# Six softmax stages of a two-layer graph network taken in pairs, by Strassen's scheme

## The chip, the cores and the metric

The kernel runs on one core of a Trainium2 chip. The metric is device time in microseconds (us), as the median of some runs. PE is TensorE, DVE VectorE, ACT ScalarE, POOL GpSimd, and SP the engine that only issues DMAs; POOL and ACT issue DMAs too. PEld is the load of a matmul's stationary operand, which PE does beside its matmuls.

## The reference, cut to what matters

There are N = 2048 nodes, a batch of B = 8 and C = 64 features. A layer multiplies the features with N x N matrices ("supports"), mixes the results with weights that differ from node to node, adds the input and normalises. The change is in the last support of layer 1:

```
apt = jax.nn.softmax(jax.nn.relu(node_embeddings @ node_embeddings.T), axis=1)
x_g = jnp.einsum('knm,bmc->bknc', supports, x)     # supports = [I, lap, 2 lap lap - I, apt]
out = jnp.einsum('bnki,nkio->bno', x_g, weights) + bias
```

So apt is a 2048 x 2048 matrix that is made on the chip, and it is multiplied with x of layer 1, which is 2048 x 512 (B times C columns). Everything is in 32-bit floats.

## The kernel before

**Stages.** The work is 5 phases (A0, B0, A1, Z1, V1) of 8 stages each, one stage for NB = 256 nodes, numbered 0 to 39 (line 680). A0 and B0 make layer 0; A1 multiplies adj with x; **Z1, stages 24 to 31, multiplies apt with x**; V1 multiplies adj with A1's result u. In most stages of the other phases the product is made by Strassen's scheme in Winograd's form (`strassen`, line 457): the 256 nodes are two halves of 128, the 2048 inner indices are two interleaved halves, the 512 columns two halves, and seven products of half size stand in place of eight, with sums T1 to T4 of x's quarters (made once, `Sums`, line 645) and sums of the matrix's quarters. A Z1 stage, and the first stages of some phases, are made plainly.

**A Z1 stage.** `scores` (line 601) makes two of the 16 blocks of 128 x 256 entries at a time: two small matmuls (tile ps) of the embeddings s1 with the stage's own embeddings e2; a DVE instruction that takes the greater of 0 and the score and subtracts a node's constant c (128x512); and ACT's exponential. The result p is a numerator of the softmax. `turned` (line 554) then runs 16 x 2 x 2 = 64 matmuls, in the profile pz<-p,x, with x's 128 columns as the stationary operand and p (128x256) as the moving one. Each stage's last step, `turned_half` (line 575), takes the two accumulators out of PSUM into the tile t with four DVE instructions (64x512) that also multiply by the reciprocal of the softmax's sum, the second row of c. Then POOL stores t's upper half (zd). V1's stages read it back later.

**The order of the work.** PE runs its instructions as the program writes them, and so does every other engine. `put(n, place, f)` (line 694) hangs a function on stage n at a place between 0 and 64 of its product; a place is scaled by the stage's length (64 for a Z1 stage; 56 for a Strassen stage, whose `yield`s sum to that). The loop at line 791 draws matmuls from the stage's generator and runs each function when its place is reached. In the Z1 stages the functions are few: scores (line 782), `load_e` of the next stage (line 772; POOL loads e2 in two DMAs and then c), the splitting of weights for V1 (lines 712 to 715, stages 25 to 28: ACT loads, DVE splits, POOL stores to wd), and `load_u` of one block of A1's result into the room u (line 728, place 12, on SP's queue).

**Rooms.** x and u are 16 slabs of 512 floats per partition each. During A1 the room u holds the sums T1 to T4 of x; in Z1 the result u is loaded over them. w_room has 16384 floats per partition for the weights of one stage; from the last use in stage 24 (place 43) to the first weights of stage 32 (place 4) it is empty. e2 and t have two buffers each, c has two, the tile group f2k four. PSUM has two accumulators of one bank (ps_acc) and three two-bank tiles (big) for everything else.

**Queues.** SP's queue holds, in program order, the loads of adj (a), of u, and of the split weights (wst, three buffers, `Ahead` at line 221). A DMA that must wait holds those behind it. In stage 32 the first weights' matmuls (pw<-e,wst) come at place 4.

Of the kernel before, what the change touches and what calls it, by code (L numbers as in the profile page):

```python
# [1 line left out]

# [12 lines left out]
P = 128  # L15
# [32 lines left out]
def two_graph_layers(ctx: ExitStack, tc: tile.TileContext, x, x_t, adj_b, adj_q, layers, out):  # L48
# [40 lines left out]
    def big(name):  # L89
        return ps_big.tile([P, 2, 512], F32, tag="big", name=name)  # L90
# [170 lines left out]
    class Stage:  # L261
        def __init__(self, n, phase, j):
            self.n, self.phase, self.j = n, phase, j
            self.li, self.kk = int(phase[1]), int(phase[0] != "A")
            self.half = phase == "B0"
            self.plain = (phase, j) in plain
            self.length = 64 if self.plain or phase == "Z1" else 56
            self.units = C // 2 if self.half else C
            self.e2 = e2[n % 2]
            self.t = self.sq = None  # L270
            self.dev = {}


        def load_e(self):
            cols = slice(self.j * NB, (self.j + 1) * NB)
            for h in range(2):
                pool.dma_start(out=self.e2[64 * h:64 * h + 64, :].bitcast(F32), in_=estk[self.li][:, cols])
            if self.phase == "Z1":
                self.c = two.tile([P, 2, NB], F32, tag="c", name="c")
                pool.dma_start(out=self.c, in_=cd[self.j].rearrange("k s p -> k (s p)").partition_broadcast(P))  # L280

        def load_acc(self):
# [127 lines left out]


        def product(self):
            if self.phase == "Z1":
                return self.turned(X, self.softmax())
            if self.kk:
                return self.turned(U, self.loaded()) if self.plain else self.strassen(U)
            if self.n == 0:
                self.slabs = U[0:SB]
            else:
                made = one.tile([P, SB, BC], F32, tag="wraw", name="u")  # L420
                self.slabs = [made[:, s, :] for s in range(SB)]
            return self.straight(X) if self.plain else self.strassen(X)
# [34 lines left out]
        def strassen(self, right):  # L457
            half = BC // 2
            k_slab = NJ // 2
            sums = self.sums  # L460
            rights = {"B11": lambda k: right[2 * k][:, 0:half], "B21": lambda k: right[2 * k + 1][:, 0:half],
                      "B22": lambda k: right[2 * k + 1][:, half:BC]}
            for i in range(4):
                rights[f"T{i + 1}"] = lambda k, i=i: sums[i](k)
            temps = one.tile([P, 4, half], F32, tag="wsplit", name="temps")
            p1, p4, v = (temps[:, i, :] for i in range(3))
            made, mine = {}, {}
            inside = self.phase == "A0"

            def quarter(name):  # L470
                mine[name] = adj.next()
                adj.held += 1

            def sum_of_a(i, name, a, b, op):
                dve.tensor_tensor(mine[name], mine[a], mine[b], op=op)
                pool.dma_start(out=sd[self.j][i].rearrange("p k n -> p (k n)"), in_=mine[name])

            def times(name, what, left):
                made[name] = acc = self.accumulator(name)[:, 0:half]
                a = (mine[left] if inside else adj.next()).rearrange("p (k n) -> p k n", n=P)  # L480
                for k in range(k_slab):
                    if self.kk:
                        for q in range(2):
                            pe.matmul(acc[:, q * P:(q + 1) * P], rights[what](k)[:, q * P:(q + 1) * P], a[:, k, :],
                                      start=(k == 0 and q == 0), stop=(k == k_slab - 1 and q == 1))
                            yield 0.5
                    else:
                        pe.matmul(acc, a[:, k, :], rights[what](k), start=(k == 0), stop=(k == k_slab - 1))
                        yield 1
                if inside and name in ("p7", "p6", "p5", "p3"):  # L490
                    adj.held -= 1
                    adj.fill()
                    self.used(what)

            def add(dst, a, b, op=ALU.add):

                if not isinstance(dst, tuple):
                    dve.tensor_tensor(dst, a, b, op=op)
                elif self.kk == 0:
                    dve.tensor_tensor(self.slabs[dst[0]][:, dst[1] * half:(dst[1] + 1) * half], a, b, op=op)  # L500
                else:
                    to = self.features()[0:64, dst[0] * P:(dst[0] + 1) * P, :]
                    for par in range(2):
                        of = lambda x: x[64 * par:64 * par + 64, :].rearrange("p (q n) -> p n q", n=P)
                        dve.tensor_tensor(to[:, :, 4 * dst[1] + par:4 * dst[1] + par + 3:2], of(a), of(b), op=op)

            if inside:
                quarter("A11")
                quarter("A22")
            yield from times("p1", "B11", "A11")  # L510
            act.copy(p1, made["p1"])
            if inside:
                quarter("A21")
                sum_of_a(2, "A11", "A11", "A21", ALU.subtract)
                sum_of_a(0, "A21", "A21", "A22", ALU.add)
            yield from times("p4", "T4", "A22")
            self.used("T4")
            act.copy(p4, made["p4"])
            if inside:
                quarter("A12")  # L520
                sum_of_a(1, "A22", "A22", "A11", ALU.subtract)
            yield from times("p7", "T3", "A11")
            add(v, made["p7"], p1)
            add(p4, v, p4, ALU.subtract)
            yield from times("p2", "B21", "A12")
            add((0, 0), made["p2"], p1)
            if inside:
                sum_of_a(3, "A12", "A12", "A22", ALU.subtract)
            yield from times("p6", "T2", "A22")
            add(v, made["p6"], v)  # L530
            add(p1, made["p6"], p1)
            add((1, 0), made["p6"], p4)
            yield from times("p5", "T1", "A21")
            add(p1, made["p5"], p1)
            add((1, 1), made["p5"], v)
            self.repeat(1)
            yield from times("p3", "B22", "A12")
            add((0, 1), made["p3"], p1)
            self.repeat(0)
            self.store_u()  # L540

        def used(self, what):

            first = {"T4": 0, "T1": 4, "T2": 8, "T3": 12}.get(what)
            if (self.phase, self.j) == ("A0", NBLK - 1) and first is not None:
                load_u(range(first // 2, min(first // 2 + 2, NBLK - 1)))

        def repeat(self, s):

            if self.half:  # L550
                t = self.t[:, s * P:(s + 1) * P, :]
                pool.dma_start(out=t[64:128, :, :], in_=t[0:64, :, :])

        def turned(self, stationary, moving):
# [13 lines left out]
                        self.turned_half(i, accs[i])  # L568
                m0 += len(group)
            if self.phase == "Z1":  # L570
                pool.dma_start(out=zd[self.j], in_=self.t[64:128, :, :])
            for s in range(SB):
                self.repeat(s)

        def turned_half(self, i, acc):
            t = self.features()
            for par in range(2):
# [5 lines left out]
                                      op=ALU.mult)  # L583
                else:
                    copy(par, t[0:64, :, at], src)

        def load_z(self):
            pool.dma_start(out=self.features()[64:128, :, :], in_=zd[self.j])
# [12 lines left out]
        def scores(self, c):  # L601
# [8 lines left out]
                                     op0=ALU.max, op1=ALU.subtract)  # L610
            act.activation(p.rearrange("p m n -> p (m n)"), p.rearrange("p m n -> p (m n)"), AF.Exp)
            self.p[c] = p


        def scores_of_rows(self, s, h):
# [56 lines left out]
    for phase, slabs, room, n in (("B0", u_all, w_room[:, 10240:16384], 3), ("A1", x_all, flat_u, 4),  # L672
                                  ("V1", u_all, flat_x, 3)):
        r = thirds(room, n)
        sums[phase] = Sums(slabs, [r[1], r[2], r[3], r[0]] if n == 4 else [r[0], None, r[1], r[2]])
    sums["A0"] = sums["A1"]

# [1 line left out]
              for j in range(NBLK)]  # L681
    for st in stages:
        st.sums = sums.get(st.phase)
    stages[0].load_e()

    split_rooms = [lambda: one.tile([P, 8, P], F32R, tag="wsplit", name="wsplit"),
# [23 lines left out]
        for part in range(3):  # L710
            put(2 + n, 24 + 5 * part, split_weights, part, *key)
    for c in range(V0 // 8):
        put(25 + c, 10, load_weights, 1, 1, c)
        for part in range(3):
            put(25 + c, 40 + part, split_weights, part, 1, 1, c)
    for i, place in ((0, 51), (3, 54), (2, 60)):
        put(8, place, sums["B0"].make, i)
    put(9, 0, sums["B0"].make, 1)
# [6 lines left out]
    for i, place in ((0, 10), (2, 20), (3, 30)):  # L725
        put(32, place, sums["V1"].make, i)
    put(33, 0, sums["V1"].make, 1)
    for j in range(NBLK):
        put(24 + j, 12, load_u, (j,))

    for n, st in enumerate(stages):
        phase = st.phase
        cuts = (0, 3, 6, 9, 12, 14, 16) if st.units == C else (0, 3, 6, 8)
# [35 lines left out]
            for k, place in enumerate(posts):  # L769
                put(n + 1, place, st.post, k)  # L770
        if n + 1 < len(stages):
            put(n, 44 if n < 23 else 37 if n < 25 else 4, stages[n + 1].load_e)
        if phase[0] == "A":
            put(*((1, 12) if n == 0 else (n, 28) if st.li == 0 else (n, 37)), st.bias)
            if st.li == 0:
# [2 lines left out]
                put(n, 47 if st.j else 57, st.turn, 0, "x")  # L778
        if phase != "Z1":
            put(*((1, 26) if n == 0 else (n, 48 + 6 * st.li) if st.kk == 0 else (n, 30)), st.load_acc)  # L780
        else:
            st.p = [None] * 8
            for c in range(8):
# [75 lines left out]
```

## Time and profile before

| | |
|---|---|
| median of 3 runs | 1505.93 us (1505.57 to 1506.24) |
| the profiled execution's own time | 1506.8 us |
| its span in the profile | 1505.0 us |
| mean granted clock of PE | 0.994 |
| PE busy from 931 to 1181 us (stages 24 to 31) | 249.98 of 250 us |
| DVE busy in the same stretch | 93.25 us |
| PE busy from 1181 us to the end | 310.15 of 324 us |
| matmuls pz<-p,x (the Z1 product) | 1024 records, 232.7 us |

A matmul on 32-bit floats shows as two records: 8 stages of 64 matmuls make the 1024. A row of the groups has the shapes, the count, then the group's busy time and the mean duration of one in ns, and then the idle time of the engine before them with what ended it. Durations of matmuls overlap, so what one costs is read from start to start. The chain of waits walks back from the last instruction to what released each step, and lists the time that each piece adds.

### The profile page before, as it was taken

To read this page: it belongs to the slowest core of one execution; us is meant where nothing else is said; L and a number is where in the kernel's file an instruction comes from. 1 tells how busy PE (TensorE), PEld (TensorE's weight loads), DVE (VectorE), ACT (ScalarE), POOL (GpSimd) and SP (SyncE) were. 2 spreads that over 40 slices of the span, in tenths; PEclk is the share of its full clock that TensorE was granted. 3 is DMA by queue.
4 is the path that set the end of the run, shared out by engine and by line. 5 is a ranking of instruction groups with operands and counts; after the bars stand their busy time and mean duration, and the time that the engine had idled before them with its cause. 6 is when DMAs were issued, how large, how long until landed. Compare 5 with 4: busy or idle time off the path is not lost.

```text
span 1505.0 us, 31332 instructions
## 1 busy us (share of the span) xinstructions
PE 1472.4 (98%) x13406; PEld 1200.7 (80%) x13406; DVE 895.1 (59%) x1599; ACT 475.6 (32%) x608; POOL 206.6 (14%) x343
## 2 busy tenths in 40 slices
PE   9999999999999999999999999999999999999996
PEld 4477777778998898477777777788888888888885
DVE  3876666628666666866666667533432466666665
ACT  1344444431221122144444444311111233333332
POOL 4222222110111111111110111110010000000100
PEclk9999999999999999999999999999999999999998
DMA  9888898874666566478887788532211346656651
GB/s 360 264 265 269 276 281 273 289 285 145 201 201 200 189 206 219 132 182 191 208 179 197 203 175 185 163 106 67 81 41 27 102 152 195 195 194 189 196 194 56
DMA packets 86732, 283.39 MB, mean 188 GB/s; under 512 B 14017, under 2 KB 18113, under 8 KB 84993
## 3 DMA queue, kind: packets, MB, share of 16 engines
q1 hardware_dynamic: 53600, 171.99, 38.5%
q0 software_dynamic: 27520, 95.76, 21.2%
q10 hardware_dynamic: 5472, 13.63, 2.7%
q8 instruction: 106, 1.74, 0.5%
q14 instruction: 34, 0.27, 0.1%
HBM read 216.28 MB, written 60.83 MB: 184 GB/s over the span
## 4 chain that ended last, share of the span: by engine, by line
PE 75%; issue 17%; DVE 3%; POOL 2%; DMA 2%; ACT 1%; POOLq 0%; ACTq 0%; DVEq 0%
PE p L42 34%; PE pz L42 18%; PE po L42 10%; PE pw L42 8%; PE pu L42 2%; DMA x<-in_x 1%; PE pt L42 1%; PE ps L42 1%; PE pr L42 1%; DVE acc L42 1%; DVE w L42 1%; POOL x1d L42 1%; DMA u<-in_w 1%; POOL t L42 1%; DVE wsplit L42 1%
## 5 line engine op out<-in xcount | busy, mean ns | idle before, releaser
L42 ACT ACTIVATE w<-pw 128x1024 f32<-128x1024 f32 x328 | 318.3, 1021 | 369.6 <-PE pw L42 366.8
L42 DVE SCALAR_TENSOR_TENSOR acc<-po,mask,acc 128x256 f32<-128x256 f32 (+1 forms) x640 | 247.0, 427 | 83.7 <-PE po L42 71.0
L42 PE MATMUL pz<-p,x 128*128 128x256 f32 x1024 | 232.7, 380 | 0.0
L42 DVE COPY w<-pw 128x1024 f32<-128x1024 f32 x120 | 146.9, 1224 | 139.4 <-PE pw L42 138.2
L42 PE MATMUL p<-a,u 128*128 128x128 f32 x1792 | 219.4, 278 | 4.4 <-PE p L42 4.1
L42 PEld LDWEIGHTS p<-a,u 128*128 128x128 f32 x1792 | 206.6, 192 | 15.2 <-PE p L42 5.1
L42 PE MATMUL po<-w,t 128*32 128x256 f32 (+1 forms) x5120 | 206.1, 337 | 7.3 <-issue 6.3
L42 PEld LDWEIGHTS pz<-p,x 128*128 128x128 f32 x1024 | 189.3, 190 | 24.2 <-issue 0.6
L42 PE MATMUL p<-u,a 128*128 128x256 f32 x832 | 203.6, 387 | 0.0
L42 PEld LDWEIGHTS po<-w,t 128*32 128x32 f32 (+1 forms) x5120 | 125.8, 108 | 81.2 <-issue 15.4
L42 PEld LDWEIGHTS p<-u,a 128*128 128x128 f32 x832 | 152.0, 190 | 29.7 <-issue 5.4
L42 PE MATMUL p<-x,a 128*128 128x256 f32 x624 | 152.6, 385 | 0.0
L42 PE MATMUL pw<-e,wst 64*128 64x256 f32 x1728 | 146.0, 296 | 1.2 <-ACT w L42 1.1
L42 PEld LDWEIGHTS pw<-e,wst 64*128 64x128 f32 x1728 | 112.1, 184 | 41.8 <-issue 21.6
L42 PEld LDWEIGHTS p<-x,a 128*128 128x128 f32 x624 | 114.2, 190 | 19.0 <-issue 0.7
L42 DVE SCALAR_TENSOR_TENSOR p<-ps,c 128x512 f32<-128x512 f32 x64 | 44.3, 691 | 119.6 <-PE ps L42 119.1
L42 ACT ACTIVATE p<-p 128x512 f32<-128x512 f32 x64 | 40.1, 629 | 181.5 <-DVE p L42 181.5
L42 PE MATMUL pu<-x,a 128*128 128x512 f32 x192 | 91.5, 624 | 1.8 <-DMA x<-x1d 1.8
L42 PE MATMUL p<-a,x 128*128 128x128 f32 x672 | 83.0, 278 | 0.1
L42 PE MATMUL p<-a,w 128*128 128x128 f32 x672 | 81.3, 277 | 0.0
L42 PEld LDWEIGHTS p<-a,x 128*128 128x128 f32 x672 | 77.8, 192 | 3.0 <-issue 0.2
L42 PEld LDWEIGHTS p<-a,w 128*128 128x128 f32 x672 | 77.3, 192 | 2.5 <-issue 1.4
(110 smaller groups left out, 1135.3 us busy)
## 6 DMA issues: line engine op xcount, KB each, us to landing
wst<-wd SPq DMA_DIRECT2D x108, 512.0 KB, 6.2
a<-in_adj_q SPq DMA_DIRECT2D x87, 512.0 KB, 5.1
a<-sd SPq DMA_DIRECT2D x84, 512.0 KB, 3.9
sd<-a POOLq DMA_DIRECT2D x24, 512.0 KB, 6.2
a<-in_adj_b SPq DMA_DIRECT2D x16, 512.0 KB, 6.9
bx<-bx POOLq DMA_DIRECT2D x32, 256.0 KB, 6.6
acc<-bx POOLq DMA_DIRECT2D x16, 512.0 KB, 5.8
pd<-acc POOLq DMA_DIRECT2D x16, 512.0 KB, 4.7
```

What stands on the lines that cost most here:

```text
L42: return self._tc.keep_in_program_order(f(*args, **kwargs))
```

## The change

Stages 24 and 25 stay as they were. Stages 26 to 31 become three pairs; each pair is one matrix of 512 nodes and is multiplied by `strassen`, with 256 nodes in a half. The even stage draws the first 56 matmuls of the 112 and the odd stage the rest.

- The numerators of a pair are made ahead, in places written out by hand, and lie in one half of w_room (pairs alternate between the halves): per stage two quarters of 8 blocks, each made by two calls of `numerators` (four score matmuls, one DVE instruction and one exponential on 128x1024) and one of `normalize` (a DVE multiplication of 128x2048 by the sum's reciprocal). `turned_half`'s multiplication falls away for these stages; Strassen's additions take its place, and four DVE sums of quarters (128x2048, in place) per pair.
- The sums T1 to T4 of x are those of A1, still in the room u. So u is loaded later: two blocks each time a product of the last pair has used up one of the four sums.
- `load_e` of these stages moves to other places; c of stage 25 lies in another buffer; the splitting of weights moves by one stage.

```diff
             self.plain = (phase, j) in plain
-            self.length = 64 if self.plain or phase == "Z1" else 56
+            self.wide = phase == "Z1" and j >= 2
+            self.length = 64 if self.plain or phase == "Z1" and j < 2 else 56
...
         def product(self):
+            if self.wide:
+                if self.j % 2 == 0:
+                    self.rest = self.pair[1].rest = self.strassen(X)
+                    return islice(self.rest, self.length)
+                return self.rest
...
+            if self.wide:
+                p1, p4, v = (four.tile([P, BC], F32, tag="f2k", name="temp") for _ in range(3))
+                mine = {f"A{h + 1}{t + 1}": self.pair[h].quarters[t] for h in range(2) for t in range(2)}
...
+            nodes = NB if self.wide else P
+            streamed = self.phase == "A0"
+            inside = streamed or self.wide
...
             def times(name, what, left):
-                made[name] = acc = self.accumulator(name)[:, 0:half]
-                a = (mine[left] if inside else adj.next()).rearrange("p (k n) -> p k n", n=P)
+                made[name] = acc = self.accumulator(name)[:, 0:2 * nodes]
+                a = (mine[left] if inside else adj.next()).rearrange("p (k n) -> p k n", n=nodes)
...
-            if (self.phase, self.j) == ("A0", NBLK - 1) and first is not None:
-                load_u(range(first // 2, min(first // 2 + 2, NBLK - 1)))
+            if (self.phase, self.j) in (("A0", NBLK - 1), ("Z1", NBLK - 2)) and first is not None:
+                load_u(range(first // 2, min(first // 2 + 2, NBLK - 1 + self.li)))
...
+        def numerators(self, t, part):
+            ps = big("ps").rearrange("p a (m n) -> p (a m) n", n=NB)
+            for i in range(4):
+                m = 2 * (4 * part + i) + t
+                pe.matmul(ps[:, i, :], s1[:, m * P:(m + 1) * P], self.e2, start=True, stop=True)
+            p = self.quarters[t][:, part * 1024:(part + 1) * 1024]
+            dve.scalar_tensor_tensor(p.rearrange("p (m n) -> p m n", n=NB), ps, 0.0,
+                                     self.c[:, 0, None, :].to_broadcast([P, 4, NB]), op0=ALU.max, op1=ALU.subtract)
+            act.activation(p, p, AF.Exp)
+
+        def normalize(self, t):
+            p = self.quarters[t].rearrange("p (m n) -> p m n", n=NB)
+            dve.tensor_tensor(p, p, self.c[:, 1, None, :].to_broadcast([P, NJ // 2, NB]), op=ALU.mult)
...
+    for n in range(26, 32, 2):
+        for h in range(2):
+            stages[n + h].pair = stages[n:n + 2]
+            room = w_room[:, 8192 * (n // 2 % 2) + 4096 * h:]
+            stages[n + h].quarters = [room[:, 2048 * t:2048 * (t + 1)] for t in range(2)]
...
-        put(25 + c, 10, load_weights, 1, 1, c)
+        put(26 + c, 10, load_weights, 1, 1, c)
         for part in range(3):
-            put(25 + c, 40 + part, split_weights, part, 1, 1, c)
+            put(26 + c, 40 + part, split_weights, part, 1, 1, c)
...
-    for j in range(NBLK):
-        put(24 + j, 12, load_u, (j,))
...
-            put(n, 44 if n < 23 else 37 if n < 25 else 4, stages[n + 1].load_e)
+            if n < 25 or n > 30:
+                put(n, 44 if n < 23 else 37 if n < 25 else 4, stages[n + 1].load_e)
...
+        elif st.wide:
+            first, even, odd = (n - 2, (16, 24, 32), (40, 48, 56)) if n % 2 == 0 else (n - 2, (28, 36, 44), (4, 12, 20))
+            load = (n - 2, 4) if n % 2 == 0 else (n - 3, 20)
+            if n == 26:
+                first, even, odd, load = 25, (4, 10, 18), (20, 26, 34), (24, 40)
+            elif n == 27:
+                first, even, odd, load = 25, (56, 61, 67), (42, 48, 54), (25, 33)
+            put(*load, st.load_e)
+            for t, places in enumerate((even, odd)):
+                for i, place in enumerate(places):
+                    at = (first, place) if place < 64 else (first + 1, place - 64)
+                    put(*at, *((st.numerators, t, i) if i < 2 else (st.normalize, t)))
```

More of the change, by code (lines that the diff above doesn't have):

```diff
@@ L1 @@
 from contextlib import ExitStack
+from itertools import islice
 import concourse.bass as bass
@@ L278, in load_e @@
             if self.phase == "Z1":
-                self.c = two.tile([P, 2, NB], F32, tag="c", name="c")
+                self.c = (one.tile([P, 2, NB], F32, tag="wsplit", name="c") if self.j == 1
+                          else two.tile([P, 2, NB], F32, tag="c", name="c"))
                 pool.dma_start(out=self.c, in_=cd[self.j].rearrange("k s p -> k (s p)").partition_broadcast(P))
@@ L464, in strassen @@
                 rights[f"T{i + 1}"] = lambda k, i=i: sums[i](k)
[L465 to L468, printed above, removed]
+            if self.wide:
+                p1, p4, v = (four.tile([P, BC], F32, tag="f2k", name="temp") for _ in range(3))
+                mine = {f"A{h + 1}{t + 1}": self.pair[h].quarters[t] for h in range(2) for t in range(2)}
+            else:
+                temps = one.tile([P, 4, half], F32, tag="wsplit", name="temps")
+                p1, p4, v = (temps[:, i, :] for i in range(3))
+                mine = {}
+            made = {}
+            nodes = NB if self.wide else P
+            streamed = self.phase == "A0"
+            inside = streamed or self.wide
             def quarter(name):
-                mine[name] = adj.next()
-                adj.held += 1
+                if streamed:
+                    mine[name] = adj.next()
+                    adj.held += 1
             def sum_of_a(i, name, a, b, op):
                 dve.tensor_tensor(mine[name], mine[a], mine[b], op=op)
-                pool.dma_start(out=sd[self.j][i].rearrange("p k n -> p (k n)"), in_=mine[name])
+                if streamed:
+                    pool.dma_start(out=sd[self.j][i].rearrange("p k n -> p (k n)"), in_=mine[name])
             def times(name, what, left):
-                made[name] = acc = self.accumulator(name)[:, 0:half]
-                a = (mine[left] if inside else adj.next()).rearrange("p (k n) -> p k n", n=P)
+                made[name] = acc = self.accumulator(name)[:, 0:2 * nodes]
+                a = (mine[left] if inside else adj.next()).rearrange("p (k n) -> p k n", n=nodes)
                 for k in range(k_slab):
@@ L483, in times @@
                         for q in range(2):
-                            pe.matmul(acc[:, q * P:(q + 1) * P], rights[what](k)[:, q * P:(q + 1) * P], a[:, k, :],
-                                      start=(k == 0 and q == 0), stop=(k == k_slab - 1 and q == 1))
-                            yield 0.5
+                            pe.matmul(acc[:, q * nodes:(q + 1) * nodes], rights[what](k)[:, q * P:(q + 1) * P],
+                                      a[:, k, :], start=(k == 0 and q == 0), stop=(k == k_slab - 1 and q == 1))
+                            yield nodes / NB
                     else:
@@ L490, in times @@
                 if inside and name in ("p7", "p6", "p5", "p3"):
-                    adj.held -= 1
-                    adj.fill()
+                    if streamed:
+                        adj.held -= 1
+                        adj.fill()
                     self.used(what)
@@ L501, in add @@
                 else:
-                    to = self.features()[0:64, dst[0] * P:(dst[0] + 1) * P, :]
+                    if self.wide:
+                        to = self.pair[dst[0]].features()[64:128, :, :]
+                    else:
+                        to = self.features()[0:64, dst[0] * P:(dst[0] + 1) * P, :]
                     for par in range(2):
-                        of = lambda x: x[64 * par:64 * par + 64, :].rearrange("p (q n) -> p n q", n=P)
+                        of = lambda x: x[64 * par:64 * par + 64, :].rearrange("p (q n) -> p n q", n=nodes)
                         dve.tensor_tensor(to[:, :, 4 * dst[1] + par:4 * dst[1] + par + 3:2], of(a), of(b), op=op)
@@ L544, in used @@
             first = {"T4": 0, "T1": 4, "T2": 8, "T3": 12}.get(what)
-            if (self.phase, self.j) == ("A0", NBLK - 1) and first is not None:
-                load_u(range(first // 2, min(first // 2 + 2, NBLK - 1)))
+            if (self.phase, self.j) in (("A0", NBLK - 1), ("Z1", NBLK - 2)) and first is not None:
+                load_u(range(first // 2, min(first // 2 + 2, NBLK - 1 + self.li)))
         def repeat(self, s):
+            if self.wide:
+                self.pair[s].store_z()
             if self.half:
@@ L570, in turned @@
             if self.phase == "Z1":
-                pool.dma_start(out=zd[self.j], in_=self.t[64:128, :, :])
+                self.store_z()
             for s in range(SB):
@@ L585, in turned_half, with store_z @@
                     copy(par, t[0:64, :, at], src)
+        def store_z(self):
+            pool.dma_start(out=zd[self.j], in_=self.t[64:128, :, :])
         def load_z(self):
@@ L675, in two_graph_layers @@
         sums[phase] = Sums(slabs, [r[1], r[2], r[3], r[0]] if n == 4 else [r[0], None, r[1], r[2]])
-    sums["A0"] = sums["A1"]
+    sums["A0"] = sums["Z1"] = sums["A1"]
     stages = [Stage(8 * i + j, phase, j) for i, phase in enumerate(("A0", "B0", "A1", "Z1", "V1"))
```

## The prediction

> **What bounds the kernel now.** First the page's busy times, then the chain of waits inside stage 25, then the busy times by stretch.
>
> ```profile
> PE 1472.4 (98%) x13406; PEld 1200.7 (80%) x13406; DVE 895.1 (59%) x1599; ACT 475.6 (32%) x608; POOL 206.6 (14%) x343
> ```
>
> PE is busy nearly throughout, so only what shortens PE's row of work, or stops it, moves the end. The chain in Z1 (start, length, what):
>
> ```profile
> 1008.90 3.45 PE pz L42 x16
> 1012.36 0.23 PE ps L42 x2
> 1012.59 3.45 PE pz L42 x16
> 1016.04 0.23 PE ps L42 x2
> ```
>
> 16 records of pz (8 matmuls) take 3.45 us and a pair of score matmuls 0.24, with nothing between: a stage is 8 x 3.687 = 29.5 us of pure PE. One record is 0.2155 us; a matmul, which I call a unit below, is two, 0.431. The other engines in one such stage (columns: PE, PEld, DVE, ACT, POOL busy, PE's clock, DMA share, GB/s):
>
> ```profile
> 1004.59:1034.08 29.49, 29.49 (x145) 26.18 (x144) 11.76 (x17) 5.04 (x8) 2.70 (x5) 1.00 0.31 85
> ```
>
> DVE is busy 11.8 of 29.5 us and the clock is full. There is room for DVE work here, and none on PE.
>
> **Removed from PE.** A pair had 128 units and has 7 x 8 x 2 = 112. Three pairs lose 48 units, 96 records: 96 x 0.2155 = **20.7 us**. I take the same record for Strassen's products, whose shapes are the same (128x128 stationary, 256 moving); the p<-x,a of A1 run 16 in 3.46 us. The scores stay as many, but come in fours: a pair took 0.239, of which 2 x 0.107 is the moving of 256 columns (half of pz's record, since a score matmul is one record), so a change of kind costs 0.026; 24 fewer changes give 0.6. Sum of the gain: **21.3 us**.
>
> **Added on DVE and ACT, beside PE.** Per pair, with durations from DVE's rows of these sizes: 8 score operations of 1024 at 1.22 (the row of w<-pw and of sq<-pr) 9.8 us; 4 normalisations and 4 sums of quarters of 2048 at 2.28 (row x<-u) 18.2; Strassen's additions, 5 of 512 and 8 of 64x512, at 0.69 (row t<-pz) 9.0; two splittings of weights at 3.6, 7.1. That is 44 of the pair's 112 x 0.431 + 8 x 0.45 = 52 us: it fits, and costs nothing as long as each deadline holds. Sum A11-A21 starts when p1 ends and is needed by p7, a product (6.9 us) later; the accumulator of each product is needed two products on. The tightest place is the end of the pairs with stages 27 and 29: in p5 DVE has 2.8 of additions, 2.4 of scores, 3.6 of splitting and 2.3 of normalising, 11.1 us in 7.8, so p5's accumulator is released 5.4 us after p5's end, against 6.9 at which the next pair's p1 wants it. The cover is 1.5 us; beyond it PE waits microsecond for microsecond. ACT (5.0 us a stage) has room.
>
> A rule against this: the Trainium skill, "SBUF — State Buffer", SBUF: two separate sides, says that a DVE operation with two SBUF inputs contends with GpSimd's reads, and that some DVE modes keep descriptors from being written. The row: POOL issued acc<-pd at 1185.04 in 0.57 us beneath a DVE sum of 2.29 that began at 1184.98. So I add nothing; by the rule taken at its worst, 2.3 us at each of the three loads below, 6.9 in all.
>
> **Moved: `load_e`.** Here I see new waits. The numerators of a later stage are matmuls in PE's row, and PE takes nothing past them; they need e2. POOL issues, in order: the last stage's zd, e2 twice, c. Stage 29's end in the timeline, and the same DMAs with the us from issue to landing:
>
> ```profile
> 1124.69 0.54 POOL L42 DMA_DIRECT2D zd<-t  x1 [27.35 <-DVE t L42]
> 1125.22 1.04 POOL L42 DMA_DIRECT2D e<-ed  x2
> 1126.25 0.58 POOL L42 DMA_DIRECT2D c<-cd  x1
> ```
> ```profile
> zd<-t POOLq DMA_DIRECT2D x1, 512.0 KB, 4.2
> c<-cd POOLq DMA_DIRECT2D x1, 256.0 KB, 5.0
> e<-ed POOLq DMA_DIRECT2D x2, 64.0 KB, 5.2
> ```
>
> Over Z1, e2 lands 4.6 to 5.6 us after issue; I take 5.1, the second e2 starting 0.53 after the first. Until now the scores stood 36 places later, so this was hidden. Three places no longer hide it:
> - *Stage 28* (load at 4, numerators at 16; 56 units, so unit 14). zd waits for the pair's last additions and goes out 1.9 us after the stage's start (1181.08 to 1182.97 at the end of stage 31), the second e2 at +2.95, landed at +8.05. PE arrives at 14 x 0.431 = 6.03. Wait **2.0**.
> - *Stage 26*, the same places, behind stage 25's zd. A score operation of 1.22 us now lies between the two halves of that stage's `turned_half` (place 61), so zd goes at about +2.35 and e2 is landed at +8.5. Wait **2.5**.
> - *Stage 25*, load at 33: e2 is free only when the scores of place 32 are done, about 0.9 us after their start; second e2 at +1.4, landed +6.5. PE arrives at place 42 after 0.43 + 10 x 0.431 = 4.74. Wait **1.8**.
>
> Sum 6.3. Behind the waiting matmuls stand the products and nothing else on PE; DVE's score operation waits for c 0.5 us longer, which delays p1's sums by some 2 us of the 6.9 they have. All e2 loads of the run landed in 2.9 to 7.3 us: at the low end the three waits are 0, at the high end 12.9. The other loads have over 10 us.
>
> **Moved: `load_u`.** SP now holds the last two blocks until p5 of the last pair has ended, and behind them, in order, the fourth adj tile and the three wst that were loaded long before. The first pw of stage 32 wants wst 16 + 4 units later, 8.6 us. SP's issues are 0.43 (u) and 0.33, so wst starts at about +1.6, the fourth of four 512 KB loads. The page has 6.2 from issue to landing for wst and 9.5 for u; between them, 7.8, gives +9.4: wait **0.8**. From both sides: none (a lone load can take 3.1), or with the longest wst, 12.1, 5.1. U itself is safe: blocks 2 and 3 are wanted 16 units into stage 32.
>
> **The clock.** What a wait of 2 us does afterwards is in the first stages and in B0: the idle time before a group, in brackets, and the clock in the stretch behind it (the column after POOL's).
>
> ```profile
> 40.45 0.82 PE L42 MATMUL pw<-e,wsplit 64*128 64x256 f32 x8 [2.06 <-DVE w L42]
> ...
> 509.70 1.75 PE L42 MATMUL po<-w,t 64*32 64x128 f32 x105 [1.64 <-issue]
> ```
> ```profile
> 42.00:43.00 1.00, 1.00 (x2) 0.34 (x1) 1.00 (x1) 0.93 (x2) 0.00 (x0) 0.50 0.17 70
> ...
> 511.00:513.00 2.00, 2.00 (x46) 1.80 (x30) 2.00 (x9) 0.00 (x0) 0.00 (x0) 1.00 0.03 8
> ```
>
> After 2.06 us idle the clock read 0.50, 0.50, 0.50, 0.81 in the four microseconds from 41: 1.7 us lost again. After 1.64 it stayed at 1.00. My waits of 1.8, 2.0 and 2.5 straddle that; I count one drop, for the longest: **1.7**. Bounds 0 and 3 x 1.7 = 5.1.
>
> The Trainium skill, "TensorE: Matmul & The Clock Gate", Why this matters for your kernels, asks only that there be no gaps over about 3 us. The row with 2.06 is harder than that. By the rule there would be no drop, and a forecast 1.7 us lower.
>
> **Sum.** -20.7 - 0.6 + 6.3 + 0.8 + 1.7 = -12.5 us. The rows are of an execution of 1506.8 us (span 1505.0, 1.8 around it), 0.9 above the median of 1505.93. From the median: **1493.4 us**.
>
> **Rivals.**
> - *The waits are hidden after all* (e2 lands in about 3 us, as the fastest did): only the gain remains, 1505.9 - 21.3 = 1484.6. For it: zd and little else moves in these stretches (31% DMA share). Against: seven stages in a row show 4.6 or more. Chance 0.14.
> - *Every wait costs the clock too, and wst comes late*: 6.3 + 5.1 + 2.5 of cost, net -7.4, 1498.5. For it: the half clock after 2.06 us. Against: 1.64, 1.49 and 1.09 left it alone. Chance 0.16.
> - *Slower: the room as one whole.* If a product that reads one half of w_room waited until the numerators just written into the other half were done, each of the 16 `numerators` calls and 8 normalisations inside stages 26 to 29 would hold PE: 16 x (1.22 + 1.15 exponential + 0.5) + 8 x 2.3 = 64 us against 21.3, giving 1549. It decides from 8 such calls of 16 on. Against it: in B0 the weights are written into the lower part of w_room while PE multiplies sums in the upper part, and that row has no idle time:
>
> ```profile
> L42 PE MATMUL p<-a,w 128*128 128x128 f32 x672 | 81.3, 277 | 0.0
> ```
>
>   Chance 0.04.
> - *DVE misses its deadlines* by about 1 us at most of the 21 products: 1503 to 1506, no change. Its tightest cover is 1.5 us, elsewhere 3 or more. Chance 0.03.
>
> That it would not multiply less is excluded by the count of products in the code.
>
> **How the numbers follow.** The forecast has 0.63; with its two neighbours 0.93. The forecast's own bounds are a landing of 4.6 to 5.6 (1.5 us either way), wst from 0 to 2.5, and none to two drops: 1489 to 1498. Over 8 in 10 the range reaches to the hidden case below and to the late case above, **1484 to 1500**, leaving out the two last rivals and a little. 0.2% is 3 us, about what a measurement of this kernel can tell: faster 0.93, same 0.03, slower 0.04.
>
> **What would show it.** In the profile after: 256 records of pz<-p,x (stages 24 and 25 alone) and 672 of p with 256 columns in Z1, 16 of them in 3.45 us; idle time of PE before ps, about 2 us each, three times, ended by the DMA of e; a short one before the first pw of stage 32, ended by wst; the clock at 0.5 for 3 us behind one or more. No idle time of PE before p that DVE ends. Wrong would be: PE waiting inside the products, idle before ps under 0.5 us, or Z1's p at over 0.23 us a record.

## The result, and the profile after

The changed kernel takes **1491.29 us** (median of 4 runs, 1487.82 to 1495.92) against 1505.86 before (4 runs, 1505.57 to 1506.24): a ratio of **0.9905**, 95% interval 0.9877 to 0.9933. So 14.6 us were gained where 12.5 were forecast; 1493.4 was 2.1 us too high. The profiled execution of after took 1492.28 us (span 1490.5). In after's trace the kernel's line is L43 where it was L42.

The page's busy times, to be held against those of before: PE has 96 records and 19.4 us less, DVE 59.5 us more.

```profile
PE 1453.0 (97%) x13310; PEld 1182.8 (79%) x13310; DVE 954.6 (64%) x1614; ACT 474.1 (32%) x590; POOL 207.4 (14%) x343
```

All of it lies between two marks: stage 25's first score matmuls at place 0, and stage 32's first product (pz<-a,u). I call this **the stretch**, and compare kernels over it, since what comes ahead of it differs by a few us from profile to profile, for a reason that was not found (last section). Before's stretch, by the busy times in one window (columns as in the prediction), and then after's:

```profile
975.09:1181.08 205.99, 205.99 (x1004) 182.53 (x1003) 70.39 (x98) 34.03 (x54) 16.65 (x31) 1.00 0.21 59
```
```profile
975.45:1166.65 191.20, 187.70 (x908) 165.55 (x907) 129.65 (x113) 32.25 (x36) 15.13 (x28) 0.99 0.27 78
```

The stretch shrank by 14.79 us. DVE's work grew from 70 to 130 us there. PE, which had no idle time, now has 191.20 - 187.70 = 3.50. Where that is, stands in after's timeline of PE (in brackets: idle time before the group, and what ended it):

```profile
996.63 0.82 PE L43 MATMUL ps<-e,s 128*128 128x256 f32 x4
...
1016.42 0.71 PE L43 MATMUL ps<-e,s 128*128 128x256 f32 x4 [2.00 <-DMA e<-ed]
...
1071.98 0.71 PE L43 MATMUL ps<-e,s 128*128 128x256 f32 x4 [1.50 <-DMA e<-ed]
...
1168.47 0.97 PE L43 MATMUL pw<-e,wst 64*128 64x256 f32 x12
```

Of the four waits forecast, two are there: stage 26's (2.00 us) and stage 28's (1.50). Stage 25's scores (first row) and stage 32's weights (last row) did not wait. The chain of waits through stage 28 shows how such a wait comes about, and the price of a product after it:

```profile
1066.71 0.52 POOL e L43
1067.23 4.61 DMA e<-ed
1071.84 0.14 issue
1071.98 0.71 PE ps L43 x4
1072.69 3.02 PE p L43 x14
```

From POOL's second issue to PE's start the chain leaves PE; then 14 records of a product take 3.02 us: 0.2157 each, what a record of pz cost before.

### The profile page after: what moved, and what is told of

It reads as the page before. It is cut to its first block, busy times and chain, and to the rows that moved or that the text cites. A ratio compares the mean times of both kernels' runs of the same rounds, so it can differ in the third digit from the quotient of the medians.

```text
span 1490.5 us, 31130 instructions
## 1 busy us (share of the span) xinstructions
PE 1453.0 (97%) x13310; PEld 1182.8 (79%) x13310; DVE 954.6 (64%) x1614; ACT 474.1 (32%) x590; POOL 207.4 (14%) x343
## 3 DMA queue, kind: packets, MB, share of 16 engines
q8 instruction: 105, 1.72, 0.5%
## 4 chain that ended last, share of the span: by engine, by line
PE 70%; issue 20%; DVE 3%; POOL 3%; DMA 3%; ACT 1%; POOLq 0%; ACTq 0%; DVEq 0%
PE p L43 40%; PE po L43 11%; PE pw L43 8%; PE pz L43 6%; PE pu L43 2%; PE pt L43 1%; DMA x<-in_x 1%; DVE w L43 1%; PE pr L43 1%; DVE acc L43 1%; PE ps L43 1%; POOL e L43 1%; POOL x1d L43 1%; DMA u<-in_w 1%; POOL t L43 1%
## 5 line engine op out<-in xcount | busy, mean ns | idle before, releaser
L43 ACT ACTIVATE w<-pw 128x1024 f32<-128x1024 f32 x328 | 318.5, 1021 | 391.6 <-PE pw L43 388.9
L43 DVE SCALAR_TENSOR_TENSOR acc<-po,mask,acc 128x256 f32<-128x256 f32 (+1 forms) x640 | 247.0, 426 | 82.7 <-PE po L43 70.0
L43 DVE COPY w<-pw 128x1024 f32<-128x1024 f32 x120 | 146.9, 1224 | 140.7 <-PE pw L43 139.4
L43 PE MATMUL p<-a,u 128*128 128x128 f32 x1792 | 219.4, 278 | 4.4 <-PE p L43 4.1
L43 PEld LDWEIGHTS p<-a,u 128*128 128x128 f32 x1792 | 206.6, 192 | 15.2 <-PE p L43 5.1
L43 PE MATMUL po<-w,t 128*32 128x256 f32 (+1 forms) x5120 | 206.1, 337 | 6.1 <-issue 5.0
L43 PE MATMUL p<-u,a 128*128 128x256 f32 x832 | 203.6, 387 | 0.0
L43 PEld LDWEIGHTS po<-w,t 128*32 128x32 f32 (+1 forms) x5120 | 125.9, 108 | 80.0 <-issue 14.0
L43 PEld LDWEIGHTS p<-u,a 128*128 128x128 f32 x832 | 152.0, 190 | 29.7 <-issue 5.4
L43 PE MATMUL p<-x,a 128*128 128x256 f32 x624 | 152.6, 385 | 0.0
L43 PE MATMUL pw<-e,wst 64*128 64x256 f32 x1728 | 146.0, 296 | 1.2 <-ACT w L43 1.1
L43 PEld LDWEIGHTS pw<-e,wst 64*128 64x128 f32 x1728 | 112.1, 184 | 41.8 <-issue 21.6
L43 PEld LDWEIGHTS p<-x,a 128*128 128x128 f32 x624 | 114.2, 190 | 19.0 <-issue 0.7
L43 PE MATMUL pu<-x,a 128*128 128x512 f32 x192 | 90.5, 617 | 3.6 <-DMA x<-x1d 2.1
L43 PE MATMUL p<-w,u 128*128 128x256 f32 x384 | 87.5, 384 | 0.0
L43 PE MATMUL p<-a,x 128*128 128x128 f32 x672 | 82.9, 278 | 0.0
L43 PE MATMUL p<-a,w 128*128 128x128 f32 x672 | 81.3, 277 | 0.0
L43 PEld LDWEIGHTS p<-w,u 128*128 128x128 f32 x384 | 73.2, 193 | 9.8
L43 PEld LDWEIGHTS p<-a,x 128*128 128x128 f32 x672 | 77.7, 192 | 2.8
L43 PEld LDWEIGHTS p<-a,w 128*128 128x128 f32 x672 | 77.3, 192 | 2.5 <-issue 1.4
L43 DVE TENSOR_TENSOR temps<-p,temps 128x256 f32<-128x256 f32 x108 | 43.1, 420 | 44.4 <-PE p L43 43.7
L43 PEld LDWEIGHTS pu<-x,a 128*128 128x128 f32 x192 | 35.5, 193 | 45.1 <-issue 36.1
```

The source lines that it names most:

```text
L43: return self._tc.keep_in_program_order(f(*args, **kwargs))
```

## The experiments

**The theory.** The scheme gives its 96 records in full; what it loses is PE standing before e2, because the load is issued behind the last stage's store; idle time of about 2 us may halve the clock. **Rivals:** the DVE work that the scheme adds costs PE time; or the rearrangement around it (numerators ahead, rooms, later `load_u`) costs or gains by itself. Expectations are quoted as they were written. The first four kernels were timed beside each other, the kernel before at a median of 1509.68 us (17 runs, 1506.38 to 1514.83); the last three likewise, with before at 1507.26 (7 runs, 1506.22 to 1509.48).

### The changed kernel again (e0_same)

No edit.

> The changed kernel once more, for its spread and its waits. Four runs of it lay between 1487.8 and 1495.9 us, of the kernel before between 1505.6 and 1506.2. Theory A (the spread and the cost come from the waits for e2 near 2 us, each of which loses 1.7 us more where the clock halves): median about 1491, spread of 4 us or more, and the mean clock lower in the slower runs. Rival B (the four runs were an accident of the first chip job): all runs within 1 us.

Measured: 1494.53 us (6 runs, 1490.25 to 1496.61), ratio 0.9898 (0.9882 to 0.9915). Its stretch is 190.21. In its timeline of PE:

```profile
1015.58 0.71 PE L43 MATMUL ps<-e,s 128*128 128x256 f32 x4 [2.28 <-DMA e<-ed]
...
1069.43 0.71 PE L43 MATMUL ps<-e,s 128*128 128x256 f32 x4 [1.49 <-DMA e<-ed]
...
1116.12 7.15 PE L43 MATMUL p<-w,x 128*128 128x256 f32 x32 [0.36 <-DVE t L43]
```

The two waits for e2 return, at the same places. New is 0.36 us at the start of stage 30, where PE waits for DVE to release an accumulator. The clock stayed at 1.00 though the first wait was longer than after's 2.00, which had halved it; the last section has the reason. The median is 3.2 us above the changed kernel's first one, as that of the kernel before is by 3.8; the spread of 6.4 us is as expected, but the next experiment shows that it does not come from the waits.

### e2 loaded earlier (e1_early)

```diff
+            if n in (28, 30):
+                load = (n - 3, 44 if n == 28 else 8)
             put(*load, st.load_e)
```

The loads of two stages now stand, in POOL's queue, ahead of the store that they stood behind.

> Loads of e2 and c of stages 28 and 30 put 2.5 to 3 us and more ahead of the zd that they stood behind (stage 25 place 44, stage 27 place 8). Theory A: no wait before ps in stages 26 and 28, no half clock in Z1; 96 records of 0.2155 less, 21 product changes of 0.03 more and 0.2 gained on the scores leave 20.2 us, so 1485.7, with a spread of 1 to 2 us. Rival B (the spread comes from something else in the pairs, DVE or DMA): the median falls only by the two waits of the profile, 3.9 us, to about 1487.5, and the spread stays at 4 us or more.

Measured: 1489.65 us (5 runs, 1485.86 to 1492.13), ratio 0.9868 (0.9849 to 0.9886). By busy times over the stretch, and POOL's order in the timeline:

```profile
974.82:1160.19 185.37, 185.37 (x908) 164.66 (x907) 129.51 (x113) 32.34 (x36) 15.09 (x28) 1.00 0.28 80
```
```profile
992.34 1.06 POOL L43 DMA_DIRECT2D e<-ed  x2 [14.71 <-PE ps L43]
...
993.95 1.04 POOL L43 DMA_DIRECT2D e<-ed  x2
...
1010.11 0.54 POOL L43 DMA_DIRECT2D zd<-t  x1 [14.27 <-DVE t L43]
```

The rows of e are the loads for stages 27 and 28. Stage 28's (the second row) is issued 16 us before stage 25's zd; stage 30's, at 1032.33, is 29 us before the zd that it stood behind (1061.61). PE is busy for all of the 185.37 us, and the stretch is 205.99 - 185.37 = **20.62** under before's. 96 records at 0.2155 are 20.69. So the waits come from the place of the load, and without them the scheme gives its records in full. After's stretch is 5.83 longer: 3.50 idle; 2 x 0.24 for the restarts, since four score matmuls take 0.71 after a wait and otherwise add 0.47; 1.7 at half clock; 0.15 left over. That rest lies at the start of stage 30, where in after two records begin 0.32 and 0.29 us after the one before them, and where e0_same has its wait for DVE. The median is 20.0 us below the kernel before, where 20.2 was expected. The spread is 6.3 us, where 1 to 2 were expected: there Rival B was right, and the spread comes from something else.

### Everything but the scheme (e2_plain)

On e1_early: a pair's stages are multiplied plainly, 64 matmuls each, from the same numerators made ahead in the same rooms; DVE copies the result out in place of Strassen's additions, and u is loaded at place 12 as before.

```diff
             if self.wide:
-                if self.j % 2 == 0:
-                    self.rest = self.pair[1].rest = self.strassen(X)
-                    return islice(self.rest, self.length)
-                return self.rest
+                q = [x.rearrange("p (k n) -> p k n", n=NB) for x in self.quarters]
+                return self.turned(X, [[q[0][:, k, :], q[1][:, k, :]] for k in range(NJ // 2)])
...
-            if self.wide:
-                self.pair[s].store_z()
...
-                if self.phase == "Z1":
+                if self.wide:
+                    dve.tensor_copy(t[64:128, :, at], src)
+                elif self.phase == "Z1":
...
+    for j in range(NBLK):
+        put(24 + j, 12, load_u, (j,))
```

> As e1_early (loads early), but stages 26 to 31 multiplied plainly, block by block, 64 matmuls a stage, with numerators made ahead, normalised in place and accumulators copied out; u loaded early as before the change. Theory A (the scheme's fewer products are the whole gain): 96 records more, 21 product changes less, so 20.0 us above e1_early, 1505.7. Rival C (making numerators ahead in fours and normalising ahead gains or costs by itself): more than 1 us away from that on either side.

Measured: 1510.34 us (10 runs, 1507.76 to 1512.21), ratio 1.0003 (0.999 to 1.0017): no difference from before. Its timeline of PE has the multiplications as pz again; the last 320 records take 69.24 us, 0.2164 each.

Its stretch is 207.25, 21.88 above e1_early's; the medians differ by 20.7, where 20.0 was expected. So Theory A holds to 0.7 us by the medians, but the stretch is 1.9 above, more than the 1 us that was to decide against it. By the stretch this form is 1.26 slower than the kernel before: 0.48 is a wait of PE for DVE early in stage 26, and about as much again is lost in short hesitations at the starts of six stages, where a record begins 0.29 us after the one before. The rearrangement without the scheme thus gains nothing and costs at most 1.3 us, and the scheme is the gain.

### More DVE work where it is tightest (e3_more_dve)

On e1_early: one DVE instruction over 128x2048 more (the greater of a quarter and itself) at place 45 of stages 27 and 29, that is in p5 of the pairs' ends.

```diff
+    def more(q):
+        dve.tensor_tensor(q, q, q, op=ALU.max)
+    for n in (27, 29):
+        put(n, 45, more, stages[n + 2].quarters[0])
```

> As e1_early, with one DVE operation of 2.28 us more (the greater of a quarter and itself, which changes nothing) in p5 of the first and second pair. The prediction's cover of 1.5 us: PE waits 0.8 us at the start of stages 28 and 30, 1.6 us in all above e1_early. By the trace after (p5's accumulator released 6.3 to 6.8 us after p5's end, against 6.9): cover 0.1 to 0.6, so 1.7 to 2.2 us each, 3.4 to 4.4 in all. Rival D (DVE hidden beyond one product): no change.

Measured: 1492.47 us (4 runs, 1490.84 to 1495.41), ratio 0.9884 (0.9864 to 0.9905); stretch 189.24, 3.87 above e1_early's, where the prediction's cover would have given 1.6:

```profile
1067.28 6.28 PE L43 MATMUL p<-w,x 128*128 128x256 f32 x28 [1.66 <-DVE t L43]
...
1121.37 7.14 PE L43 MATMUL p<-w,x 128*128 128x256 f32 x32 [1.72 <-DVE t L43]
```

An instruction of 2.29 us makes PE wait 1.66 and 1.72, so the cover was about 0.6 by the idle time, and 0.4 by what the stretch lost. DVE's work is hidden, but only just; I had put the cover at 1.5.

### e2 wanted six places sooner (e4_longer)

On the changed kernel: the first numerators that are made in stages 26 and 28 (for stages 28 and 30) stand at place 10 instead of 16. Places of these stages are scaled by 56/64, so that is 5 matmuls in the trace, 2.16 us earlier.

```diff
-            first, even, odd = (n - 2, (16, 24, 32), (40, 48, 56)) if n % 2 == 0 else (n - 2, (28, 36, 44), (4, 12, 20))
+            first, even, odd = (n - 2, (10, 24, 32), (40, 48, 56)) if n % 2 == 0 else (n - 2, (28, 36, 44), (4, 12, 20))
```

> The changed kernel with the first numerators of stages 28 and 30 at place 10 instead of 16, so PE arrives 5.25 units, 2.26 us, sooner at matmuls whose e2 is loaded no sooner. The profiles of the changed kernel showed waits of 2.0 to 2.3 us (stage 26) and 1.5 us (stage 28), in all some 3.7. Theory A: now 4.2 to 4.6 and 3.7 to 3.8, and from stage 25 to stage 32 the stretch is 185.4 (as in e1_early, without waits) + 8.4 = 193.8 if the clock stays full, + 1.7 for each place where it halves. If idle time alone decides, both places must halve (197.2), since 2.0 us did it once; if it also hangs on something that differs between runs (2.28 us did not in the second profile), one or none can.

Measured in a single run: 1501.2 us; stretch 199.02, 13.65 above e1_early's.

```profile
1017.78 1.19 PE L43 MATMUL ps<-e,s 128*128 128x256 f32 x4 [4.43 <-DMA e<-ed]
...
1077.20 0.71 PE L43 MATMUL ps<-e,s 128*128 128x256 f32 x4 [4.30 <-DMA e<-ed]
```

The waits grew by 2.43 and 2.80 over after's: 2.16 because the scores come sooner, the rest because the second e2 landed 4.45 and 5.26 us after its issue, where after had 4.18 and 4.61. Wanting e2 sooner did not bring it sooner. Of the 13.65, 8.73 are waits, 0.5 restarts, and the rest the clock: after the first wait PE worked 5.7 us at half speed (2.8 lost), after the second 3.4 (1.7). The doubled first drop was not expected.

### A store ahead of stage 25's load (e5_ahead)

On e1_early: a store of 512 KB from w_room to spare memory directly ahead of the load that had not waited.

```diff
+    spare = dram.tile([P, 1024], F32, tag="spare", name="spare")
+    put(25, 32.5, lambda: pool.dma_start(out=spare, in_=stages[26].quarters[1][:, 1024:2048]))
```

> e1_early with a spare store of 512 KB put on POOL's queue straight ahead of e2's load at stage 25, place 33, where the prediction had a wait of 1.8 us and none came (e2 landed 2.5 us after issue, nothing was ahead of it). Theory A (what stands ahead on POOL's queue makes e2's 4.3 to 5.6 us): the second e2 lands 4.3 us or more after issue, and PE waits 1 to 2.5 us before the scores of place 42. Rival B (the landing depends on the place and the load of that moment, not on the store ahead): about 2.5 us again, no wait.

Measured in a single run: 1490.14 us; stretch 186.96, 1.59 above e1_early's. PE's timeline, and then the DMA issues in that window (KB each, median us to landing):

```profile
1000.71 0.71 PE L43 MATMUL ps<-e,s 128*128 128x256 f32 x4 [1.36 <-DMA e<-ed]
```
```profile
e<-ed POOLq DMA_DIRECT2D x4, 64.0 KB, 4.5
```

With a store ahead the two halves of this load land 4.1 and 4.6 us after issue (the view's 4.5 is the median of them and of the two of the load behind), and PE waits 1.36. So the store ahead is what makes the load late; whether by its place in the queue or by the traffic that it makes, this run does not separate. In after, where nothing is ahead of it, the same view gave:

```profile
e<-ed POOLq DMA_DIRECT2D x2, 64.0 KB, 2.5
```

### Early loads, and less DVE work at the pairs' ends (e6_relief)

On e1_early: the splitting of weights moves to place 58 in odd stages, away from p5, and the first weights of stage 32 are loaded at place 4 of stage 30.

```diff
-            put(26 + c, 40 + part, split_weights, part, 1, 1, c)
+            put(26 + c, (58 if c % 2 else 40) + part, split_weights, part, 1, 1, c)
...
+    put(30, 4, wst.fill)
```

> e1_early, with the two splittings of the odd stages moved from p5's to p3's share of the time (place 58), and the weights of stage 32 loaded ahead of u. Theory A (nothing else is left in Z1 to take away): the stretch from stage 25 to stage 32 is 185.0 to 185.4, no wait on DVE at the pairs' ends, and the time equal to e1_early's, about 20 us under the kernel before. Rival: DVE's work in p3 delays the last additions and costs up to 1 us.

Measured: **1485.82 us** (4 runs, 1483.94 to 1490.29), ratio 0.9867 (0.9849 to 0.9885). The stretch is 185.37, e1_early's to the hundredth, without any wait of PE. It is faster than the kernel before; the changed kernel was not timed beside it, but its stretch was 4.8 to 5.8 us longer. Over e1_early no gain can be told, since none of what it relieves was late there. What it buys is margin where e0_same showed 0.36 us of waiting: the additions that release p5's accumulator end 3.1 and 3.0 us before p1 begins in stages 28 and 30, against 0.6 in e1_early.

## Why the prediction was right, and where it was off

The mechanism and the sum held; single terms did not. That the sum came out within 2.3 us is in part luck: four waits were put 3.6 us too high together, and 1.2 us of the other terms were missed the other way. For the profiled execution of after:

| term | forecast | measured | by |
|---|---|---|---|
| 96 records less | -20.7 | -20.6 | e1_early against before |
| scores in fours | -0.6 | 0 | a four 0.47, two pairs 2 x 0.23 |
| stage 28's wait | 2.0 | 1.50 | timeline |
| stage 26's wait | 2.5 | 2.00 | timeline |
| stage 25's wait | 1.8 | none | timeline, e5_ahead |
| wst in stage 32 | 0.8 | none | timeline |
| clock | 1.7 | 1.7 | windows |
| restarts and rest | - | 0.6 | after against e1_early |
| sum | -12.5 | -14.8 | stretch |

**Removed from PE: right.** The record's duration carried over to products out of w_room. The 0.6 for fewer changes between products and scores was mis-sized: a change does not cost the 0.026 that I took for the remainder of a pair. e1_early's 20.62 leaves nothing for it.

**Moved, `load_e`: right in kind, too high three times.** Stage 25 is the step that failed most: "All e2 loads of the run landed in 2.9 to 7.3 us", and I took 5.1 for all three. That was the mean of rows in which the load stood directly behind a zd. Stage 25's load has no store ahead, and landed in 2.5; e5_ahead put one there and the 4.5 us and the wait came back. No e2 load of before landed that soon: the low end of my range, 2.9 (at 631.85), had two copies of 256 KB directly ahead of it on POOL's queue, and the one e2 load of Z1 without a large store directly ahead (at 955.51, in stage 24) took 6.3 and 6.0 us, while four loads of u and one of adj were in flight on SP's queue. After the change those loads of u come later, and the same load, at 955.87, landed in 2.5. So the store ahead is one cause of a late landing and other traffic may be another, which no experiment tried alone. (At the low end, 2.9, stage 26 would still have waited 0.3, not 0.) In stages 26 and 28 the wait was put 0.5 too high, since the second e2 landed after 4.18 and 4.61, not 5.1; in stage 26 a later zd took back the rest. In after's POOL timeline the order is as I had it, zd at 1011.06, 2.84 us after stage 26's first product (I had 2.35), then e2; the first row is stage 25's load:

```profile
992.96 1.06 POOL L43 DMA_DIRECT2D e<-ed  x2 [14.71 <-PE ps L43]
...
1011.06 0.54 POOL L43 DMA_DIRECT2D zd<-t  x1 [16.47 <-DVE t L43]
1011.59 1.04 POOL L43 DMA_DIRECT2D e<-ed  x2
```

**Moved, `load_u`: no wait**, with 0.9 us to spare. wst went out 1.1 us after the last p5 (forecast 1.6) and landed after 6.8 (forecast 7.8), at 1167.6; PE wanted it at 1168.47.

**DVE beside PE: right that it is hidden, wrong in how well.** The cover at the pairs' ends is about 0.6 us, not 1.5, and at the end of stage 29 the changed kernel had none: there after loses 0.15 us and e0_same waits 0.36. DVE's timeline at the end of stage 27:

```profile
1056.83 2.45 DVE L43 TENSOR_TENSOR wsplit<-wraw,wsplit 32x1024 fp32r<-32x1024 f32 x2
1059.31 2.29 DVE L43 TENSOR_TENSOR w<-w,c 128x2048 f32<-128x2048 f32 x1
...
1062.23 1.39 DVE L43 TENSOR_TENSOR t<-p,temp 64x512 f32<-64x512 f32 x2
```

p5 ended at 1057.36. The rest of a splitting and a normalisation (second row) still lie ahead of its additions, which end at 1063.62, 6.3 us later; I had 5.4. Of the contention that I priced at 6.9 us at its worst nothing showed: in after POOL's store wd at 1114.03, issued beneath a DVE instruction of 2.29 us with two SBUF inputs (from 1113.77), landed after 2.91 us, and the one at 1091.00, beneath a score operation, after 2.90.

**The clock: the size was right in after by luck.** "I count one drop, for the longest" came true there (2.00 us idle, 1.7 lost), but e0_same had none after 2.28. I had gone by the length of single waits, and before's own trace speaks against that. Waits of 1.09 and 0.75 us (from 628.05 to 631.02), each shorter than the 1.64 that "stayed at 1.00", together left PE idle for 1.84 of 3.41 us, and the clock then fell (PE busy after the comma; the clock is the third column from the end):

```profile
628.05:631.46 3.41, 1.57 (x4) 0.59 (x4) 3.41 (x4) 0.00 (x0) 0.69 (x2) 1.00 0.63 255
631.46:634.88 3.42, 3.42 (x6) 1.55 (x5) 3.32 (x10) 1.11 (x1) 1.52 (x4) 0.50 0.55 192
```

The last section has the rule that these rows follow; the 1.64 lay across one of its borders (at 508.59), 0.53 and 1.11.

**Rivals.** The hidden case (1484.6) is what e1_early and e6_relief make by moving the load, not what the change does. The late case had every wait cost the clock and wst late: the first came only in e4_longer, whose waits were twice as long and more, the second in no run. DVE missed its deadline at one of the 21 products, by 0.15 us in after and 0.36 in e0_same. The room as one whole is excluded: after's PE has no wait inside a product for what DVE or ACT write into w_room.

## What to carry to other kernels

Strassen's scheme on a stage bound by PE gave its records in full here, as long as every transfer and every release of an accumulator kept its place; count the new deadlines, not the busy shares. Before a landing time is taken from a row, ask what stood ahead of the DMA in its queue there and what else was in flight, and put small urgent loads ahead of large stores in program order. Where work is pushed under PE, double one piece of it in the tightest place: the wait that appears tells what cover was left.

## What the runs showed of the hardware that was not expected

**When idle time halves the clock.** In all nine profiles of this study the clock's falls lie whole multiples of 3.4133 us apart within a profile, to 0.03 us; each profile has its own phase. So the clock is decided per window of 3.413 us, and what counts is the idle time inside one window, not the length of a wait. Three profiles cut at these windows (PE busy after the comma; the clock is the third column from the end). After, then e0_same, then e4_longer:

```profile
1014.46:1017.87 3.41, 1.45 (x9) 1.37 (x10) 0.22 (x1) 0.00 (x0) 0.35 (x1) 1.00 0.67 227
1017.88:1021.29 3.41, 3.41 (x10) 2.66 (x9) 3.38 (x3) 1.53 (x2) 0.00 (x0) 0.50 0.00 1
```
```profile
1011.31:1014.73 3.42, 2.00 (x10) 1.41 (x8) 0.33 (x1) 0.00 (x0) 2.36 (x5) 1.00 0.88 194
1014.73:1018.14 3.41, 2.56 (x14) 2.36 (x15) 1.13 (x1) 0.00 (x0) 0.00 (x0) 1.00 0.49 167
1018.14:1021.55 3.41, 3.41 (x19) 3.06 (x18) 3.38 (x3) 1.53 (x2) 0.00 (x0) 1.00 0.00 0
```
```profile
1013.22:1016.64 3.42, 0.13 (x1) 0.00 (x0) 0.63 (x1) 0.00 (x0) 2.65 (x5) 1.00 0.94 220
1016.64:1020.05 3.41, 2.27 (x8) 2.04 (x9) 1.05 (x1) 0.00 (x0) 0.00 (x0) 0.50 0.47 173
1020.05:1023.46 3.41, 3.41 (x10) 2.69 (x9) 0.18 (x1) 1.06 (x1) 0.00 (x0) 0.50 0.00 0
```

After's 2.00 us fell almost wholly into one window (1.96 idle), and the next ran at 0.50. e0_same's 2.28 fell across a border, 1.42 and 0.85, and no window slowed. e4_longer's 4.43 filled one window and took 1.14 of the next, and two windows slowed. Over the windows at full clock of all nine profiles from 25 us to 1465 us: up to 1.69 us idle the next window always kept the full clock, from 2.06 on it never did (11 of 11), and between, 7 of 10 fell. In a window already at half clock less idle time was enough to stay there: 1.14 us in e4_longer and 0.59 in e5_ahead (from 46.89); the 18 others had 0.17 or less and the clock came back. The drop so costs 1.7 us per slow window when PE is busy in it. The Trainium skill, "TensorE: Matmul & The Clock Gate", Part 1: The HAM clock gate, gives the window as 3413 ns and free-running, which these profiles confirm; it lets the clock fall after at least one idle window, and here a window about half idle was enough.

**A small load behind a large store.** In after a load of 64 KB landed 2.5 to 2.6 us after POOL's issue with nothing ahead of it (955.87 and 992.96), and 4.1 to 4.7 directly behind the 512 KB store zd on the same queue (stages 26, 28 and 30); in seven stages of before it was 4.4 to 5.8 there.

**What stays open.** Runs of one kernel differ by more than the change's small terms: 8.5 us over 17 runs of the kernel before. I had put after's spread down to its waits, and that fell: e1_early's profile has none, and its runs spread over 6.3. In the profiles the difference lies ahead of the stretch, which begins anywhere from 972.9 to 980.6 us, while what follows it takes 323.6 to 324.8 in all. Why was not tried.
